# A two-layer gated feed-forward network in float32 on one core: its small inputs packed into two arrays, and one queue for the first layer's base weights

## The chip, the cores and the metric

The kernel runs on one core of a Trainium2 chip. The metric is the device time of one execution in microseconds (us). Before the change, three runs took 442.56, 443.47 and 443.69 us; their median is 443.47 us. One further execution was recorded by the hardware profiler, and every duration below comes from that one.

## What is computed

There are eight sequences (b) of 128 tokens with 512 features. The network has two layers, and each adds its result to x. The part that the change touches is the first layer's condition: a dense product with W, and a low-rank correction by two of eight experts per token. The experts are chosen by logits to which the sequence's language adds 5.

```python
def _L0_cond_ref(x, language_ids, W, Wr, A, B):
    base = jnp.einsum('btd,od->bto', x, W)
    logits = jnp.einsum('btd,ed->bte', x, Wr)
    logits = logits + one_hot(language_ids, E)[:, None, :] * LANG_BIAS
    topw, topi = jax.lax.top_k(logits, TOP_K)
    weights = jax.nn.softmax(topw, axis=-1)
    gates = jnp.sum(jax.nn.one_hot(topi, E) * weights[..., None], axis=-2)
    h = jnp.einsum('btd,erd->bter', x, A)
    lora_out = jnp.einsum('bter,bte,eor->bto', h, gates, B)
    return base + SCALING * lora_out
...
x = x + _L0_ffn_ref(_L0_cond_ref(x, ...), ...)
x = x + _L1_ffn_ref(_L1_cond_ref(x, L1_cond_weight, itok_B_3_7), ...)
```

After the condition come a gated feed-forward with 4-bit weights (scales and zero points by groups of 128 rows), then a second layer: one 512 x 512 weight per sequence, picked by a second list of eight numbers, a root-mean-square norm with weights ln_w, and a gated feed-forward in float32.

## The kernel before, in words

The 1024 tokens are worked on in two halves of 512 columns (tb 0 and 1), features on the 128 partitions in four chunks (c, or m for outputs). A float32 product is made of three passes over parts of the operands: both operands are split into a high part and a scaled rest (x: `x_high`, `x_low`, `x_scaled`; base weights: `w_high`, `w_low`), and a third pass takes their differences (`x_diff`, `w_diff`). ScalarE (ACT) makes the high parts and the scaled rests, VectorE (DVE) the lows and differences.

**Loads.** `wa` (272 KB) holds the weights of the experts' logits and of their first factor A. `xb` is x, eight loads of 256 KB, one per sequence. `wT` holds the base weights, four loads of 256 KB, one per output chunk m. `bT` is the experts' second factor. SyncE (SP) issues `wa`, xb 1, 3, 5 and 7, the eight language numbers `ids0` between xb 3 and xb 5, then wT 0 and 2, `bT`, `shifts`, two parts of `g_idx`, `ids1`, the first quantised weights `qw`, the zero points `qz`, a second `qw`, the scales `sc` and `scd`, `ln_w`, `qzd`, and the residual `xT`. ACT issues xb 0, 2, 4 and 6 at the start (L220), and wT 1 and 3 (L708, through L226) behind `x_high(0)` in its own instruction stream.

In the built program all loads issued by SP and ACT, counted together, carry eight counters in turn. So each of these loads waits, on the engine that issues it, until the load eight places before it has landed. The order of the places before is: xb0, wa, xb2, xb1, xb4, xb3, xb6, ids0; xb5, xb7, wT0, wT2, bT, shifts, g_idx, g_idx; ids1, qw, qz, wT1, wT3, qw, sc, scd; ln_w, qzd, xT, xT, qwd.

**Order of work.** For TensorE (PE), DVE and ACT the order is written out by hand (L702 to L767). PE: `experts(0)` and `experts(1)` (logits and A products of each half), then 16 matmuls of the first base pass of half 0 (L723, four for each m, each m after its `w_high(m)`), the transposes `turned` of the gated values (L724), the second pass of half 0, two passes of half 1, and the third passes, the low-rank products (L416) and the split of the condition (L675, L676) that the gate and up products of the feed-forward read.

```python
exp0 = experts(0)
x_high(0)
for m in range(1, KC, 2):
    load_wT(m, nc.scalar)
x_low(0)
x_scaled(0)
exp1 = experts(1)
for m in range(2):
    w_high(m)
hg0 = gated(0, rows_of(exp0))
for m in range(2, KC):
    w_high(m)
```

`gated` (L306) is a chain of small DVE operations with one Exp on ACT in its middle (L325). ACT works in program order, so that Exp stands behind `w_high(1)`, and the four of `x_scaled(0)` stand behind ACT's two loads. Behind the Exp, DVE does the rest of `gated(0)`, `w_low`, `x_low(1)`, `x_diff(0)`, `w_diff`, `gated(1)`, `x_diff(1)` and the unpacking of the first quantised weights (L425, L428, L445).

A second version of the network, `in_float32` (L828), is in the program for inputs whose groups or scales are unusual; it does not run here.

Of the kernel before, what the change touches and what calls it, by code (L numbers as in the profile page):

```python
# [13 lines left out]
F32 = mybir.dt.float32  # L14
F32R = mybir.dt.float32r
I32 = mybir.dt.int32
U32 = mybir.dt.uint32
U16 = mybir.dt.uint16
# [4 lines left out]
P = 128  # L23
B, T, D = 8, 128, 512
# [40 lines left out]

LINE = 16
GU_PLACE, FLAG_PLACE, COND_PLACE = 64, 24, 48

AFTER = 0.3
FETCHED = [EngineType.PE, EngineType.DVE, EngineType.Activation]  # L70
# [21 lines left out]
def network_in(ctx, tc, a, out, by_groups, flag, again):  # L92
# [116 lines left out]
    wT3 = [cp.tile([P, KC, D], F32R, name=f"wT{i}") for i in range(3)]  # L209
    xd = [cp.tile([P, KC, TB], F32R, name=f"xd{tb}") for tb in range(NTB)]  # L210
    bT = cp.tile([P, D], F32, name="bT")
    wa = cp.tile([P, KC * (E + E * R) + COND_PLACE], F32, name="wa")
    wa = wa[:, : KC * (E + E * R)].rearrange("p (c n) -> p c n", c=KC)
    g_idx = const.tile([P, KC + NJ0], I32, name="g_idx")
    ids = const.tile([P, 2, B], I32, name="ids")
    shifts = const.tile([P, 2], U16, name="shifts")

    nc.sync.dma_start(out=wa, in_=a["WA"])
    for b in range(B):
        (nc.scalar, nc.sync)[b % 2].dma_start(  # L220
            out=xb[:, b].rearrange("p c t -> p (c t)"), in_=a["xb"][b]
        )
        if b == 3:
            nc.sync.dma_start(out=ids[:, 0, :], in_=a["ids0"].partition_broadcast(P))
    def load_wT(m, eng):
        eng.dma_start(out=wT[:, m, :], in_=a["WT"][:, m, :])  # L226

    for m in range(0, KC, 2):
        load_wT(m, nc.sync)
    nc.sync.dma_start(out=bT, in_=a["BT"])  # L230
    nc.sync.dma_start(out=shifts, in_=a["shifts"])
    nc.sync.dma_start(out=g_idx[:, :KC], in_=a["g_idx_gu"])
    nc.sync.dma_start(out=g_idx[:, KC:], in_=a["g_idx_d"])
    nc.sync.dma_start(out=ids[:, 1, :], in_=a["ids1"].partition_broadcast(P))

    def load_residual():
        for c in range(0, KC, 2):
# [15 lines left out]
    make_identity(nc, ident)  # L253
    eps = const.tile([P, 1], F32, name="eps")
    nc.gpsimd.memset(eps, RMS_EPS)
    ln_w = const.tile([P, KC], F32, name="ln_w")

    def in_range(dst, src, n, name):
        wrap = const.tile(list(src.shape), F32, name=f"wrap_{name}")
# [7 lines left out]
    def indices():  # L267
        in_range(idx[:, :KC], g_idx[:, :KC], NG_GU, "gu")
        in_range(idx[:, KC:], g_idx[:, KC:], NG_D, "d")
        lora = const.tile([P, B], F32, name="lora")  # L270
        in_range(lora, ids[:, 1, :], E, "l1")
        nc.vector.scalar_tensor_tensor(
            row1, lora, float(P), iota_p.to_broadcast([P, B]), ALU.mult, ALU.add
        )
# [31 lines left out]
    def gated(tb, banks):  # L306

        nb = TB // T
        ct = lambda shape, name, dt=F32: cp.tile(shape, dt, tag=name, bufs=2, name=name)
        logits = ct([P, nb, E], "logits")  # L310
        tok = ids[:, 0, tb * nb : (tb + 1) * nb, None]
        nc.vector.tensor_tensor(logits, tok.to_broadcast([P, nb, E]), ebc, ALU.is_equal)
        for i, ps in enumerate(banks):
            some = logits[:, 2 * i : 2 * i + 2, :]
            nc.vector.scalar_tensor_tensor(some, some, LANG_BIAS, ps[:, :, :E], ALU.mult, ALU.add)
        top = ct([P, nb, 8], "top")
        topi = ct([P, nb, 8], "topi", U32)
        for b in range(nb):
            nc.vector.max(top[:, b, :], logits[:, b, :])
            nc.vector.max_index(topi[:, b, :], top[:, b, :], logits[:, b, :])  # L320
        w = ct([P, 2, nb, 1], "w")
        dif = ct([P, nb, 1], "dif")
        ex = ct([P, nb, 1], "ex")
        nc.vector.tensor_tensor(dif, top[:, :, 1:2], top[:, :, 0:1], ALU.subtract)
        nc.scalar.activation(ex, dif, AF.Exp)  # L325
        nc.vector.tensor_scalar(dif, ex, 1.0, None, ALU.add)
        nc.vector.reciprocal(dif, dif)
        nc.vector.tensor_scalar(w[:, 0], dif, SCALING, None, ALU.mult)
        nc.vector.tensor_tensor(w[:, 1], w[:, 0], ex, ALU.mult)
        gates = ct([P, nb, E], "gates")  # L330
        second = ct([P, nb, E], "second")
        for n, g in enumerate((gates, second)):
            nc.vector.tensor_tensor(g, topi[:, :, n : n + 1].to_broadcast([P, nb, E]), ebc, ALU.is_equal)
            nc.vector.tensor_tensor(g, g, w[:, n].to_broadcast([P, nb, E]), ALU.mult)
        nc.vector.tensor_tensor(gates, gates, second, ALU.add)
        hg = ct([P, nb, E * R], "hg")
        for i, ps in enumerate(banks):
            some = slice(2 * i, 2 * i + 2)
            nc.vector.tensor_tensor(
                hg[:, some, :].rearrange("p b (e r) -> p b e r", e=E),  # L340
                ps[:, :, E:].rearrange("p b (e r) -> p b e r", e=E),
                gates[:, some, :, None].to_broadcast([P, 2, E, R]),
                ALU.mult,
            )
        return hg
# [107 lines left out]
    def by_groups_of_scales():  # L453
        gu_stack = ExitStack()
        gup = gu_stack.enter_context(tc.tile_pool(name="gup", bufs=1, side="left"))
        sc = const.tile([P, 2 * NJ0, NG_GU], F32, name="sc")
        scd = const.tile([P, KC, NG_D], F32, name="scd")
        qz = gup.tile([P, 2 * 2 * KC * NW + GU_PLACE], U16, name="qz")
        qz = qz[:, GU_PLACE:].rearrange("p (h a w) -> p h a w", h=2, a=2 * KC)
        qws, qwds, wqs, dqs, zqs, wds, h2 = {}, {}, {}, {}, {}, {}, {}  # L460
# [10 lines left out]
            out=qz.rearrange("p h a w -> p (h a w)"), in_=a["qzb_gu"].partition_broadcast(P)  # L471
        )
        load_qw(*PAIRS0[1])
        nc.sync.dma_start(out=sc, in_=a["sc_gu_T"])
        nc.sync.dma_start(out=scd, in_=a["sc_d_T"])
        nc.sync.dma_start(out=ln_w, in_=a["ln_w"])
        qzd = gup.tile([P, NJ0, P], U16, name="qzd")
        nc.sync.dma_start(
            out=qzd.rearrange("p k n -> p (k n)"), in_=a["qzb_d"].partition_broadcast(P)
# [222 lines left out]
        with tc.manual_schedule(engines={EngineType.PE, EngineType.DVE, EngineType.Activation}):  # L702
# [1 line left out]
            nc.scalar.activation(root, eps, AF.Exp)  # L704
            exp0 = experts(0)
            x_high(0)
            for m in range(1, KC, 2):
                load_wT(m, nc.scalar)  # L708
            x_low(0)
            x_scaled(0)  # L710
            exp1 = experts(1)
# [116 lines left out]
    def in_float32():  # L828
        gp_stack = ExitStack()
        ax = gp_stack.enter_context(tc.tile_pool(name="gx", bufs=1, side="left")).tile([P, KC, NT], F32, name="ax")  # L830
        load_residual()
        for m in range(1, KC, 2):
            load_wT(m, nc.scalar)
        scale_bT()
        for m in range(KC):
            for part in (w_high, w_low, w_diff):
# [86 lines left out]
                        )  # L923
                    nc.vector.tensor_tensor(xT[:, m, cols], xT[:, m, cols], ps, ALU.add)
        h_stack.close()
        nc.sync.dma_start(out=ln_w, in_=a["ln_w"])
        pools["w1"] = w1_stack.enter_context(tc.tile_pool(name="w1", bufs=1, side="right"))
        first_w1()
        open_l1()
# [312 lines left out]
def hidden_order(w, axis):  # L1242

    return by_nibbles(w, axis, [16] * KC)
# [64 lines left out]
def chunks(w):  # L1309

    return w.reshape(-1, P, w.shape[1]).transpose(1, 0, 2)
# [4 lines left out]
    return w.reshape(P, KC, KC, P).swapaxes(1, 2).reshape(P, KC, D)  # L1316


def laid_out(i):
    sc = gate_up_order(i["L0_ffn_scales_gu"])  # L1320
    sc_halves = [inner_order(h, 1) for h in (i["L0_ffn_scales_gu"][:, :INTER0], i["L0_ffn_scales_gu"][:, INTER0:])]
    sc_d = x_order(i["L0_ffn_scales_down"], 1)
    qz = pairs(i["L0_ffn_qzeros_gu"])
    qz_d = np.ascontiguousarray(pairs(i["L0_ffn_qzeros_down"])).reshape(NG_D, P)
    g_d = np.pad(inner_order(i["L0_ffn_g_idx_down"], 0), (0, P - CH0[10]), mode="edge")
    gate, up = (i[k].reshape(NJ1, P, KC, P).transpose(0, 3, 2, 1) for k in ("L1_ffn_gate_w", "L1_ffn_up_w"))
    p = np.arange(P)
    d = {
        "xT": x_order(i["x"].reshape(NT, D), 1).T,
        "xb": x_order(i["x"].reshape(NT, D), 1).T.reshape(KC, P, B, T).transpose(2, 1, 0, 3).reshape(B, P, D),  # L1330
        "ids0": i["itok_B_0_7"],
        "ids1": i["itok_B_3_7"],
        "WT": by_chunk(chunks(x_order(hidden_order(i["L0_cond_W"], 0), 1).T)),
        "WA": chunks(
            x_order(np.concatenate([i["L0_cond_Wr"], i["L0_cond_A"].reshape(E * R, D)]), 1).T
        ),
        "BT": hidden_order(i["L0_cond_B"], 1).transpose(0, 2, 1).reshape(E * R, D),
        "shifts": np.stack([4 * (p // 16 % 4), 4 * (p // 12 % 4)], axis=1).astype(np.uint16),
        "qw_gu": by_partition(gate_up_order(i["L0_ffn_qweight_gu"]), [16] * KC),
        "qz_gu0": qz[:, 0],  # L1340
        "qz_gu1": qz[:, 1],
        "qzb_gu": qz.transpose(1, 0, 2).reshape(-1),
        "sc_gu": sc,
        "sc_gu_T": np.stack([by_output(h) for h in sc_halves], axis=2).reshape(P, 2 * NJ0, NG_GU),
        "g_idx_gu": hidden_order(i["L0_ffn_g_idx_gu"], 0).reshape(KC, P).T,
        "qw_d": by_partition(x_order(i["L0_ffn_qweight_down"], 1), [n // 8 for n in CH0]),
        "qz_d": qz_d,
        "qzb_d": np.concatenate([qz_d, qz_d[-1:]]).reshape(-1),
        "sc_d": sc_d,
        "sc_d_T": by_output(sc_d),  # L1350
        "g_idx_d": g_d.reshape(NJ0, P).T,
        "w1": x_order(i["L1_cond_weight"], 2).transpose(0, 2, 1).reshape(E, KC, P, D).transpose(0, 2, 1, 3).reshape(E * P, KC * D),
        "ln_w": i["L1_ffn_ln_w"].reshape(KC, P).T,
        "wgu1": np.stack([gate, up], axis=3).reshape(NJ1, P, KC, 2 * P),
        "wd1": chunks(x_order(i["L1_ffn_down_w"], 0).T),
    }
    return {k: np.ascontiguousarray(v) for k, v in d.items()}
# [17 lines left out]
```

## Time and profile before

| | us |
|---|---|
| median of three runs | 443.47 |
| the profiled execution, its time | 444.12 |
| its span, first to last instruction | 442.3 |
| PE busy in the span | 427.3 (97%) |
| DVE busy | 302.3 (68%) |
| ACT busy | 232.0 (52%) |
| from the start to the first gate product of layer 0 | 50.6 |

The span is counted from the first instruction. Most of it is PE at work; the first 25 us are the stretch in which PE has idle time of microseconds and in which the granted clock falls to half. The DMA queues move 9.68 of the 33.07 MB in the first 60 us. A chain of waits is followed back from the last instruction; a row "DMA wT<-in_WT" in it is the time from a load's issue until it had landed, and "SPq" or "ACTq" is the issuing of a load by that engine.

### The profile page before, as it was taken

The page shows a single profiled execution, that of the slowest core. Times are in us where ns is not written, and L with a number is a line of the kernel's source. Part 1 is how long each engine was busy: PE and PEld are TensorE (multiplying, and loading weights), DVE is VectorE, ACT ScalarE, POOL GpSimd, SP SyncE. Part 2 cuts the span into 40 slices and gives each one's busy share as a digit, 9 for nine tenths or more (in the row PEclk, how much of TensorE's full clock was granted, in tenths as well). Part 3 has the DMA queues.
Part 4 walks back from the last instruction along what each step waited for, and adds up shares of the span by engine and source line. Part 5 has one row for each costly group of instructions (what it writes and reads, how often), then busy time and mean ns, then how long its engine had stood idle before and what let it go on. Part 6 is the DMA issues. An engine that isn't in the chain of part 4 may idle for free.

```text
span 442.3 us, 4852 instructions
## 1 busy us (share of the span) xinstructions
PE 427.3 (97%) x1855; PEld 335.8 (76%) x1855; DVE 302.3 (68%) x432; ACT 232.0 (52%) x269; POOL 9.0 (2%) x20
## 2 busy tenths in 40 slices
PE   8599999999999999999999999999999999999993
PEld 8486678888888866446888888888888888888882
DVE  4298979997999678867449926379626477634652
ACT  3553588867896766346487323475132471325321
POOL 0000000000000200210000000000000000000000
PEclk9799999999999999999999999999999999999997
DMA  7950130101000602870403301112001110000004
GB/s 273 282 217 0 49 96 0 49 19 37 0 0 1 272 13 97 298 270 4 142 1 104 133 1 37 47 50 94 36 0 47 49 48 24 1 0 1 1 31 163
DMA packets 13103, 33.07 MB, mean 75 GB/s; under 512 B 2705, under 2 KB 5265, under 8 KB 12049
## 3 DMA queue, kind: packets, MB, share of 16 engines
q1 hardware_dynamic: 10480, 21.68, 14.7%
q0 software_dynamic: 1152, 8.39, 5.1%
q10 hardware_dynamic: 1440, 2.62, 1.8%
q8 instruction: 16, 0.26, 0.2%
q14 instruction: 15, 0.11, 0.1%
HBM read 30.59 MB, written 2.10 MB: 74 GB/s over the span
## 4 chain that ended last, share of the span: by engine, by line
PE 82%; issue 8%; DMA 7%; ACT 1%; POOL 0%; DVE 0%; ACTq 0%; SPq 0%; POOLq 0%; DVEq 0%
PE gate L1066 17%; PE up L1066 17%; PE down L1131 17%; PE gate L544 7%; PE up L544 7%; PE down L592 7%; PE base L390 5%; DMA w<-in_w,row 3%; DMA wT<-in_WT 3%; PE adapt L1009 2%; PE base L416 2%; DMA xb<-in_xb 1%; POOL w L277 0%; DVE xT L1148 0%; PE nxT L1029 0%
## 5 line engine op out<-in xcount | busy, mean ns | idle before, releaser
L1066 PE MATMUL gate<-a,w 128*128 128x512 f32 x336 | 81.7, 390 | 0.0
L1066 PE MATMUL up<-a,w 128*128 128x512 f32 x336 | 81.4, 389 | 0.0
L1131 PE MATMUL down<-h,d 128*128 128x512 f32 x336 | 76.8, 389 | 0.0
L1066 PEld LDWEIGHTS up<-a,w 128*128 128x128 f32 x336 | 63.1, 188 | 13.1
L1131 PEld LDWEIGHTS down<-h,d 128*128 128x128 f32 x336 | 63.1, 188 | 13.1
L1066 PEld LDWEIGHTS gate<-a,w 128*128 128x128 f32 x336 | 62.7, 188 | 13.5 <-ACT gate L175 0.6
L1083 DVE SCALAR_TENSOR_TENSOR h<-up,sl 128x1024 f32<-128x1024 f32 (+1 forms) x16 | 17.5, 1091 | 50.9 <-PE up L1066 44.5
L544 PE MATMUL gate<-a,dq 128*128 128x512 f32 (+1 forms) x176 | 47.7, 393 | 0.1
L544 PE MATMUL up<-a,dq 128*128 128x512 f32 (+1 forms) x176 | 47.4, 391 | 0.0
L592 PE MATMUL down<-h,wd 128*128 128x512 f32 (+1 forms) x176 | 42.3, 394 | 0.6 <-DVE h L189 0.4
L592 PEld LDWEIGHTS down<-h,wd 128*128 128x128 f32 (+1 forms) x176 | 32.5, 188 | 9.5 <-DVE h L189 0.9
L544 PEld LDWEIGHTS gate<-a,dq 128*128 128x128 f32 (+1 forms) x176 | 32.5, 185 | 8.4 <-ACT sl L560 0.6
L544 PEld LDWEIGHTS up<-a,dq 128*128 128x128 f32 (+1 forms) x176 | 32.4, 185 | 8.0 <-DVE a L676 0.3
L199 ACT ACTIVATE h<-h 128x1024 fp32r<-128x1024 f32 (+1 forms) x25 | 26.4, 1055 | 15.9 <-DVE h L1083 15.5
L1080 ACT ACTIVATE sl<-gate 128x1024 f32<-128x1024 f32 (+1 forms) x16 | 14.7, 918 | 36.0 <-PE gate L1066 36.0
L189 DVE TENSOR_TENSOR h<-h,h 128x1024 fp32r<-128x1024 f32 (+1 forms) x25 | 30.4, 1216 | 3.4 <-ACT h L199 3.4
L175 ACT ACTIVATE gate<-gate,ratio 128x1024 f32<-128x1024 f32 (+1 forms) x24 | 26.1, 1086 | 10.6 <-PE gate L544 10.6
L175 ACT ACTIVATE gate<-gate 128x1024 f32<-128x1024 f32 (+1 forms) x15 | 13.8, 923 | 30.5 <-PE gate L1066 30.5
L1009 PE MATMUL adapt<-w,xT 128*128 128x512 f32 x64 | 28.9, 597 | 0.4 <-DMA w<-in_w,row 0.4
L175 ACT ACTIVATE down<-down 128x1024 f32<-128x1024 f32 (+1 forms) x10 | 9.2, 923 | 35.8 <-PE down L1131 35.8
L175 ACT ACTIVATE up<-up,ratio 128x1024 f32<-128x1024 f32 (+1 forms) x23 | 25.0, 1085 | 5.1 <-PE up L544 5.1
L1148 DVE SCALAR_TENSOR_TENSOR xT<-down,xT 128x1024 f32<-128x1024 f32 (+1 forms) x17 | 19.6, 1160 | 9.3 <-PE down L1131 9.1
(139 smaller groups left out, 485.9 us busy)
## 6 DMA issues: line engine op xcount, KB each, us to landing
wgu<-in_wgu SPq DMA_DIRECT2D x14, 512.0 KB, 3.3
wd<-in_wd SPq DMA_DIRECT2D x6, 512.0 KB, 3.6
qw<-in_qw_gu SPq DMA_DIRECT2D x5, 512.0 KB, 4.1
xT<-in_xT SPq DMA_DIRECT2D x2, 1024.0 KB, 6.4
xb<-in_xb ACTq DMA_DIRECT2D x4, 256.0 KB, 5.4
xb<-in_xb SPq DMA_DIRECT2D x4, 256.0 KB, 5.5
qwd<-in_qw_d SPq DMA_DIRECT2D x2, 512.0 KB, 6.0
out<-xT SPq DMA_DIRECT2D x4, 256.0 KB, 3.0
```

The source lines that it names most:

```text
L175: nc.scalar.activation(ps, ps, AF.Copy, scale=by)
L189: nc.vector.tensor_tensor(lo, x, hi.bitcast(F32), ALU.subtract)
L199: nc.scalar.activation(hi, x, AF.Copy, scale=HSCALE)
L390: nc.tensor.matmul(base[m], lhsT=wT3[i][:, m, c * P : (c + 1) * P], rhs=x_parts(tb)[i][:, c, :], start=(i == 0 and c == 0), stop=(i == 1 a ...
L544: nc.tensor.matmul(ps, lhsT=dqs[j][:, c, half, :], rhs=a3[i][:, c, tb * TB : (tb + 1) * TB], start=(c == 0 and i == 0), stop=(i == 1), ski ...
L592: nc.tensor.matmul(ps[:, tb], lhsT=wds[k][:n, m * P : (m + 1) * P], rhs=h2[k][i][:, tb], start=(first and i == 0), stop=(i == 1), skip_gro ...
L1009: nc.tensor.matmul(ps, lhsT=xT[:, c, b * T : (b + 1) * T], rhs=wt[:, c * D : (c + 1) * D], start=(c == 0), stop=(c == KC - 1),)
L1066: nc.tensor.matmul(ps, lhsT=w3[j][i][:, c, half * P : (half + 1) * P], rhs=a3[i][:, c, tb * TB : (tb + 1) * TB], start=(i == 2 and c == 0) ...
L1080: nc.scalar.activation(sl, ps, AF.Silu, scale=1.0 + EPS)
L1083: nc.vector.scalar_tensor_tensor(h, ps, 1.0 + EPS, sl, ALU.mult, ALU.mult)
L1131: nc.tensor.matmul(banks[m, tb], lhsT=d3[j][i][:, m * P : (m + 1) * P], rhs=h3[j][i][:, tb], start=(i == 0 and j == j0), stop=(j == j1 - 1 ...
L1148: nc.vector.scalar_tensor_tensor(x, ps, -EPS, x, ALU.mult, ALU.add)
```

## The change

The language numbers `ids0` are repeated on every partition and appended to `wa`'s rows, 8 words behind 544, so they come in `wa`'s load. `sc`, `scd`, `ln_w`, both parts of `g_idx`, `ids1` and `shifts` become slices of one tile `small` with one load of 156 words per partition (78 KB). The tile is 176 words wide, 704 bytes; the tiles that it replaces took 64 + 64 + 32 + 32 + 352 + 160 = 704 bytes, so the tiles above it in the pool lie where they lay. All four wT loads are issued by SP directly behind xb 7, and then `bT` and `small`; ACT issues only xb 0, 2, 4 and 6. The order on PE, DVE and ACT is otherwise the same. Packing is done in the layout of the inputs, ahead of the launch.

```diff
+SMALLS = (2 * NJ0 * NG_GU, KC * NG_D, KC, KC + NJ0, B, 1)
+SMALL = 176
...
-    wa = cp.tile([P, KC * (E + E * R) + COND_PLACE], F32, name="wa")
-    wa = wa[:, : KC * (E + E * R)].rearrange("p (c n) -> p c n", c=KC)
-    g_idx = const.tile([P, KC + NJ0], I32, name="g_idx")
-    ids = const.tile([P, 2, B], I32, name="ids")
-    shifts = const.tile([P, 2], U16, name="shifts")
-
-    nc.sync.dma_start(out=wa, in_=a["WA"])
+    wa_ids = cp.tile([P, KC * (E + E * R) + COND_PLACE], I32, name="wa")[:, : KC * (E + E * R) + B]
+    wa = wa_ids[:, : KC * (E + E * R)].bitcast(F32).rearrange("p (c n) -> p c n", c=KC)
+    ids0 = wa_ids[:, KC * (E + E * R) :]
+
+    nc.sync.dma_start(out=wa_ids, in_=a["WA"])
     for b in range(B):
         (nc.scalar, nc.sync)[b % 2].dma_start(
             out=xb[:, b].rearrange("p c t -> p (c t)"), in_=a["xb"][b]
         )
-        if b == 3:
-            nc.sync.dma_start(out=ids[:, 0, :], in_=a["ids0"].partition_broadcast(P))
-    def load_wT(m, eng):
-        eng.dma_start(out=wT[:, m, :], in_=a["WT"][:, m, :])
-
-    for m in range(0, KC, 2):
-        load_wT(m, nc.sync)
+    for m in range(KC):
+        nc.sync.dma_start(out=wT[:, m, :], in_=a["WT"][:, m, :])
     nc.sync.dma_start(out=bT, in_=a["BT"])
-    nc.sync.dma_start(out=shifts, in_=a["shifts"])
-    nc.sync.dma_start(out=g_idx[:, :KC], in_=a["g_idx_gu"])
-    nc.sync.dma_start(out=g_idx[:, KC:], in_=a["g_idx_d"])
-    nc.sync.dma_start(out=ids[:, 1, :], in_=a["ids1"].partition_broadcast(P))
+
+    small = const.tile([P, SMALL], I32, name="small")
+    nc.sync.dma_start(out=small[:, : sum(SMALLS)], in_=a["small"])
+    at = np.cumsum((0,) + SMALLS)
+    sc, scd, ln_w, g_idx, ids1, shifts = (small[:, at[i] : at[i + 1]] for i in range(len(SMALLS)))
...
-        tok = ids[:, 0, tb * nb : (tb + 1) * nb, None]
+        tok = ids0[:, tb * nb : (tb + 1) * nb, None]
...
-        nc.sync.dma_start(out=sc, in_=a["sc_gu_T"])
-        nc.sync.dma_start(out=scd, in_=a["sc_d_T"])
-        nc.sync.dma_start(out=ln_w, in_=a["ln_w"])
...
             x_high(0)
-            for m in range(1, KC, 2):
-                load_wT(m, nc.scalar)
             x_low(0)
```

More of the change, by code (lines that the diff above doesn't have):

```diff
@@ L222, in network_in @@
         )
-        if b == 3:
-            nc.sync.dma_start(out=ids[:, 0, :], in_=a["ids0"].partition_broadcast(P))
-    def load_wT(m, eng):
-        eng.dma_start(out=wT[:, m, :], in_=a["WT"][:, m, :])
-    for m in range(0, KC, 2):
-        load_wT(m, nc.sync)
-    nc.sync.dma_start(out=bT, in_=a["BT"])
-    nc.sync.dma_start(out=shifts, in_=a["shifts"])
-    nc.sync.dma_start(out=g_idx[:, :KC], in_=a["g_idx_gu"])
-    nc.sync.dma_start(out=g_idx[:, KC:], in_=a["g_idx_d"])
-    nc.sync.dma_start(out=ids[:, 1, :], in_=a["ids1"].partition_broadcast(P))
+    for m in range(KC):
+        nc.sync.dma_start(out=wT[:, m, :], in_=a["WT"][:, m, :])
+    nc.sync.dma_start(out=bT, in_=a["BT"])
+    small = const.tile([P, SMALL], I32, name="small")
+    nc.sync.dma_start(out=small[:, : sum(SMALLS)], in_=a["small"])
+    at = np.cumsum((0,) + SMALLS)
+    sc, scd, ln_w, g_idx, ids1, shifts = (small[:, at[i] : at[i + 1]] for i in range(len(SMALLS)))
+    sc = sc.bitcast(F32).rearrange("p (j g) -> p j g", j=2 * NJ0)
+    scd = scd.bitcast(F32).rearrange("p (m g) -> p m g", m=KC)
+    ln_w, shifts = ln_w.bitcast(F32), shifts.bitcast(U16)
     def load_residual():
@@ L255, in network_in @@
     nc.gpsimd.memset(eps, RMS_EPS)
-    ln_w = const.tile([P, KC], F32, name="ln_w")
     def in_range(dst, src, n, name):
@@ L270, in indices @@
         lora = const.tile([P, B], F32, name="lora")
-        in_range(lora, ids[:, 1, :], E, "l1")
+        in_range(lora, ids1, E, "l1")
         nc.vector.scalar_tensor_tensor(
@@ L455, in by_groups_of_scales @@
         gup = gu_stack.enter_context(tc.tile_pool(name="gup", bufs=1, side="left"))
-        sc = const.tile([P, 2 * NJ0, NG_GU], F32, name="sc")
-        scd = const.tile([P, KC, NG_D], F32, name="scd")
         qz = gup.tile([P, 2 * 2 * KC * NW + GU_PLACE], U16, name="qz")
@@ L831, in in_float32 @@
         load_residual()
-        for m in range(1, KC, 2):
-            load_wT(m, nc.scalar)
         scale_bT()
@@ L925, in in_float32 @@
         h_stack.close()
-        nc.sync.dma_start(out=ln_w, in_=a["ln_w"])
         pools["w1"] = w1_stack.enter_context(tc.tile_pool(name="w1", bufs=1, side="right"))
@@ L1316, in by_chunk, with each, words @@
     return w.reshape(P, KC, KC, P).swapaxes(1, 2).reshape(P, KC, D)
+def each(v):
+    return np.broadcast_to(v, (P, len(v)))
+def words(*parts):
+    return np.concatenate([np.ascontiguousarray(x).view("<i4") for x in parts], axis=1)
 def laid_out(i):
@@ L1326, in laid_out @@
     gate, up = (i[k].reshape(NJ1, P, KC, P).transpose(0, 3, 2, 1) for k in ("L1_ffn_gate_w", "L1_ffn_up_w"))
+    wa = chunks(x_order(np.concatenate([i["L0_cond_Wr"], i["L0_cond_A"].reshape(E * R, D)]), 1).T)
     p = np.arange(P)
@@ L1330, in laid_out @@
         "xb": x_order(i["x"].reshape(NT, D), 1).T.reshape(KC, P, B, T).transpose(2, 1, 0, 3).reshape(B, P, D),
-        "ids0": i["itok_B_0_7"],
-        "ids1": i["itok_B_3_7"],
         "WT": by_chunk(chunks(x_order(hidden_order(i["L0_cond_W"], 0), 1).T)),
-        "WA": chunks(
-            x_order(np.concatenate([i["L0_cond_Wr"], i["L0_cond_A"].reshape(E * R, D)]), 1).T
-        ),
-        "BT": hidden_order(i["L0_cond_B"], 1).transpose(0, 2, 1).reshape(E * R, D),
-        "shifts": np.stack([4 * (p // 16 % 4), 4 * (p // 12 % 4)], axis=1).astype(np.uint16),
+        "WA": words(wa.reshape(P, -1), each(i["itok_B_0_7"])),
+        "BT": hidden_order(i["L0_cond_B"], 1).transpose(0, 2, 1).reshape(E * R, D),
+        "small": words(
+            np.stack([by_output(h) for h in sc_halves], axis=2).reshape(P, -1),
+            by_output(sc_d).reshape(P, -1),
+            i["L1_ffn_ln_w"].reshape(KC, P).T,
+            hidden_order(i["L0_ffn_g_idx_gu"], 0).reshape(KC, P).T,
+            g_d.reshape(NJ0, P).T,
+            each(i["itok_B_3_7"]),
+            np.stack([4 * (p // 16 % 4), 4 * (p // 12 % 4)], axis=1).astype("<u2"),
+        ),
         "qw_gu": by_partition(gate_up_order(i["L0_ffn_qweight_gu"]), [16] * KC),
@@ L1343, in laid_out @@
         "sc_gu": sc,
-        "sc_gu_T": np.stack([by_output(h) for h in sc_halves], axis=2).reshape(P, 2 * NJ0, NG_GU),
-        "g_idx_gu": hidden_order(i["L0_ffn_g_idx_gu"], 0).reshape(KC, P).T,
         "qw_d": by_partition(x_order(i["L0_ffn_qweight_down"], 1), [n // 8 for n in CH0]),
@@ L1349, in laid_out @@
         "sc_d": sc_d,
-        "sc_d_T": by_output(sc_d),
-        "g_idx_d": g_d.reshape(NJ0, P).T,
         "w1": x_order(i["L1_cond_weight"], 2).transpose(0, 2, 1).reshape(E, KC, P, D).transpose(0, 2, 1, 3).reshape(E * P, KC * D),
-        "ln_w": i["L1_ffn_ln_w"].reshape(KC, P).T,
         "wgu1": np.stack([gate, up], axis=3).reshape(NJ1, P, KC, 2 * P),
```

## The prediction, made before the changed kernel was run

> **What bounds the kernel now.** I read the page first: PE is busy for 427.3 of 442.3 us, so a change of loads can only win where PE stands still or runs slowly. Then the stretches, cut where PE's work changes. Columns behind the stretch: its length, the busy time of PE, PE's weight loads, DVE, ACT, POOL, then PE's granted clock, DMA share, GB/s.
>
> ```profile
> 4.00:12.83 8.83, 8.41 (x75) 7.98 (x72) 4.37 (x20) 2.54 (x5) 0.00 (x0) 1.00 0.90 291
> 12.83:16.30 3.47, 0.00 (x0) 0.00 (x0) 0.00 (x0) 2.71 (x5) 0.00 (x0) 1.00 1.02 345
> 16.30:18.84 2.54, 1.20 (x5) 0.68 (x5) 0.00 (x0) 0.68 (x3) 0.00 (x0) 0.72 1.01 321
> 18.84:24.33 5.49, 5.49 (x14) 4.22 (x15) 5.18 (x17) 4.30 (x9) 0.00 (x0) 0.51 0.98 320
> 24.33:50.60 26.27, 26.27 (x105) 18.82 (x104) 23.60 (x70) 10.48 (x14) 0.00 (x0) 1.00 0.21 75
> ```
>
> The experts' products end at 12.83. PE then does nothing for 3.47 us, four base products and another gap, and twelve more at half clock. From 24.33 it never stops. The chain that ended last, in order of time (start, length, what), says why:
>
> ```profile
> 6.12 5.56 DMA wT<-in_WT
> 11.67 0.02 issue
> 11.69 6.44 DMA wT<-in_WT
> 18.13 0.02 issue
> 18.16 0.64 ACT wT L377
> 18.80 0.04 issue
> 18.84 5.49 PE base L390 x12
> 24.33 0.46 PE experts L410 x4
> 24.79 14.84 PE base L390 x64
> ```
>
> It runs through two base weight loads, one issued only when the other had landed. ACT's timeline shows where (start, length; in brackets the idle time before and its end):
>
> ```profile
> 7.87 0.63 ACT L359 ACTIVATE a<-xb 128x512 fp32r<-128x512 f32 x1 [1.40 <-DMA xb<-in_xb]
> 11.69 1.80 ACTq L226 DMA_DIRECT2D wT<-in_WT  x2
> 13.54 2.19 ACT L369 ACTIVATE a<-a 128x512 fp32r<-128x512 f32 x4 [5.05 <-issue]
> 15.64 0.61 ACT L377 ACTIVATE wT<-wT 128x512 fp32r<-128x512 f32 x1
> 18.16 0.63 ACT L377 ACTIVATE wT<-wT 128x512 fp32r<-128x512 f32 x1 [1.91 <-DMA wT<-in_WT]
> 18.69 0.19 ACT L325 ACTIVATE ex<-dif 128x4 f32<-128x4 f32 x1
> 20.20 0.63 ACT L377 ACTIVATE wT<-wT 128x512 fp32r<-128x512 f32 x1 [0.80 <-DMA wT<-in_WT]
> ```
>
> ACT is done with x_high(0) at 8.50, then idles 5.05 us in front of its own two loads, which wait for the loads eight places ahead (wT2, landed at 11.67; bT, issued at 8.05, landed 4.3 later at 12.35). All of x_scaled, w_high and the Exp queue behind that. DVE waits 7.7 us for the Exp (waits view).
>
> **Part 1, the base weights on SP: when they land.** In the new order ids0 leaves its place, so xb5 is eighth and goes out in the first burst near 2.1 instead of at 4.40. The rest wait eight places back, on landings worked out from issue plus time to landing: xb7 on xb0 (4.35), wT0 on wa (4.24), wT1 on xb2 (5.7), wT2 on xb1 (5.3, but SP is in order, so about 6.1), wT3 on xb4 (8.05). Before, SP's successive 256 KB loads xb7, wT0, wT2, bT landed at 10.5, 11.06, 11.67, 12.36, a step of 0.55 to 0.7. Now wT0 to wT3 follow xb7 in that row. At the old pace they land at 11.06, 11.67, 12.36, 13.0. Early bound: about 1 us sooner, because the DMA rate sags to some 190 GB/s from 6 to 8 us and xb5 can fill that. Late bound: the time that wT1 and wT3 took beside qw and qz, 6.4 and 7.8 us after issue, that is 12.2 and 15.9. I take the old pace, the nearest row: same sizes, same queue, no quantised weights beside them.
>
> **ACT.** Its two issues (1.80 us) and the wait go. x_scaled(0) follows x_high(0): 8.50 + 2.19 = 10.7 (its last input, x_low, ends at 9.22). w_high(0) 11.06 to 11.7, w_high(1) to 12.3, Exp to 12.5 (its input is ready at 11.17), w_high(2) to 13.1, w_high(3) to 13.8.
>
> **PE.** At full clock a base product takes 14.84 / 64 = 0.232 us, so from 12.83 the four groups want their weights at 12.83, 13.76, 14.69 and 15.61. They are ready at 11.7, 12.3, 13.1, 13.8: at least 1.1 us of slack each. The pass then ends at 12.83 + 16 x 0.232 = 16.54 instead of 24.33: 7.8 us. Of these, 4.8 are the two PE waits for w_high (3.5 and 1.3), and 3.0 are half clock and small gaps. The clock needs its own check. The Trainium skill, "TensorE: Matmul & The Clock Gate", section "What's actually happening", has half rate after an idle window of about 3.4 us and full rate after one busy window of that length. The trace has a gap of 3.47, half rate soon after, and full rate only near 24.2, 5.4 us into unbroken work (18.84). If a gap that size stayed, the page would price the restart at half of 3.4, 1.7 us; the row prices it at 5.49 - 12 x 0.232 = 2.7. With no gap left, I take neither: full clock, as in 4.00:12.83.
>
> **What is late next.** Behind the Exp, DVE works without a pause from 18.88 to 41.34 (22.46 us); it then waits 1.15 for ACT's split of the condition, and 0.50 before the next one at 44.22. With the Exp's end at 12.5 it is done at 35.0. PE, 7.8 earlier, lets ACT split at 33.65, and its first part is out at 34.7. DVE is 0.3 late there, and the 0.50 takes it up; up to an Exp's end of about 12.7 nothing is lost, and beyond it each us of the Exp costs PE one. ACT: the kept copy, x_high(1), scaling of bT and hgT end at about 17.8; PE wants x_high(1) at 20.7 (ready at 16.6) and x_scaled(1) at 24.4 (ready near 20.4). The hg values, 2.5 us behind the Exp, are there at 15.0, wanted at 16.54. I take 0.1 off for all this: 7.7.
>
> **Part 2, the packed inputs.** Eight loads go, one comes: SP's issue rows for the eight add up to 4.0 us (0.33 to 1.07 each), against one of about 0.45, plus 2 x 0.4 for the two wT. The skill, "DMA: Bandwidth & Descriptors", "Rules for kernel authors", calls transfers under 64 KB mostly overhead and asks for one large one; its section on the anatomy of one DMA gives about 2.0 us fixed each. By that rule seven fewer would be 14 us. The trace has 3.6 to 8.1 us from issue to landing for each, but no engine row waits for any of their contents: they overlap, and what they take is places among the eight. So in this sum they are worth nothing by themselves. What hides small: it goes out when xb6 has landed (about 9.2) and lands by 17.3 even at sc's 8.1; its first reader, shifts at 39.55, moves to about 32. Without that cover each us past 32 would cost one. wa's rows grow from 544 to 552 words, 1.5% of 3.5 us: 0.05, inside the 0.1 between wa's landing (4.24) and xb0's (4.35).
>
> **Part 3, what moves behind.** SP's row is now xb7, four wT, bT, small, qw, qz, qw, qzd, xT, qwd. Bytes are nearly the same, in less time. qz and qw took 7.2 to 8.9 us to land; issued near 10.5 to 11.5, they are there by 20, and DVE wants them at about 31.5 and 33. qwd, issued after xT, landed at 29.3 before and is wanted at 50.1. xb5 in the first burst shares engines with xb3 and xb4. xb3 stands ahead of it in SP's row, so I take no change; bounds: 0.4 earlier (PE's wait at 7.89 is 0.42) to 0.6 later (one place in the row), and either moves everything. Behind 50.6, loads wait for buffers that engines release, so they move along; nothing there gives or takes.
>
> **The sum.** Span 442.3 - 7.7 = 434.6; the profiled execution, 444.12 with 1.8 around its span, 436.4. It lay 0.65 above the median, so against the median of 443.47: 435.8.
>
> **The rivals.**
> 1. As summed: 435.8; its own range 435.0 to 436.8. Chance 0.79.
> 2. The weights stay slow, at the late bound: wT3 at 15.9, w_high(3) out at 16.5 instead of by 15.61: 0.9 lost, and 0.6 more if xb3 is late too: 437.3. For it: wT1 and wT3 did take that long. Against: qw and qz were beside them. Chance 0.10.
> 3. DVE becomes the bound. The Exp stands behind w_high(1); if wT1 lands at 13.8, 8.1 us after issue (the slowest small load's time), the Exp ends at 14.6 and 1.9 us are lost: 437.7. Chance 0.06.
> 4. It doesn't do what it says: w_high(0) still comes after 16.2, the gap is over 3.4 us and the clock falls: 443.5. Chance 0.02; wT0 would have to land 5 us later than now.
> 5. Slower: the quantised inputs starve. qz is now behind all base weights in one in-order queue, and DVE's unpacking stops until it lands. Each us after 31.5 is a us of PE's; it decides from 31.5 + 7.7 = 39.2. At 41 the time is 445.3. Against it: about 4.4 MB through qz at the 380 GB/s of busy slices are 12 us. Chance 0.03.
>
> Range: 434.6 to 437.8; it takes in cases 1 to 3. A measurement here can tell about 0.3% (1.3 us) from no change. Cases 1 to 3 are faster by more; with a little on each side, faster 0.95, same 0.02, slower 0.03.
>
> **What would show it.** Right: no wT load on ACT's queue and no idle time before L369; wT3 landed by about 13; base products unbroken from 12.83 to 16.5 at clock 1.00; first gate product near 42.8; no new PE wait for DVE before that. Wrong: a PE wait for w_high in the first pass; Exp ending after 12.7 with PE waiting for L676; xb3 landing well off 7.85; DVE waiting for qz or qw.

## The result, and the profile after

Six executions of each kernel: 443.49 us before (median, 442.56 to 444.84), 436.89 us after (436.04 to 437.84). The ratio is 0.985, 95% interval 0.9829 to 0.9871, 6.6 us less. The profiled execution after took 436.83 us, with a span of 434.9. Among the executions below, one of before (875.84 us), one of e1 (723.06) and one of e4 (1314.49) were slow; the ratios leave them out, and without them the medians of e1 and e4 are 441.71 and 442.08.

The stretches after, cut at the same times as before (columns as there: length, busy PE, PE's weight loads, DVE, ACT, POOL, granted clock, DMA share, GB/s):

```profile
4.00:12.83 8.83, 8.54 (x75) 8.34 (x73) 4.82 (x23) 6.44 (x14) 0.00 (x0) 1.00 1.01 354
12.83:16.30 3.47, 3.47 (x18) 2.83 (x18) 3.30 (x12) 3.47 (x7) 0.00 (x0) 1.00 1.02 332
16.30:18.84 2.54, 2.54 (x15) 2.08 (x14) 2.54 (x5) 1.73 (x4) 0.00 (x0) 1.00 0.92 320
18.84:24.33 5.49, 5.49 (x25) 4.44 (x24) 5.49 (x11) 3.25 (x5) 0.00 (x0) 1.00 0.99 400
24.33:50.60 26.27, 26.27 (x103) 18.51 (x103) 24.42 (x69) 11.73 (x13) 0.00 (x0) 1.00 0.19 62
```

PE is busy in every part from 12.83 on, and the clock is full. The chain that ended last (start, length, what) no longer passes a base weight:

```profile
1.65 6.56 DMA xb<-in_xb
8.21 0.04 issue
8.25 4.90 PE experts L293 x40
13.15 3.73 PE base L390 x16
16.89 0.44 PE experts L410 x4
17.33 14.83 PE base L390 x64
```

Its only load is xb3, landed at 8.21. The first base pass ends at 16.89 instead of 24.33, 7.44 us sooner, and the span is 7.4 shorter. ACT's timeline after:

```profile
8.23 0.63 ACT L359 ACTIVATE a<-xb 128x512 fp32r<-128x512 f32 x1 [1.56 <-DMA xb<-in_xb]
8.77 2.17 ACT L369 ACTIVATE a<-a 128x512 fp32r<-128x512 f32 x4
10.87 1.32 ACT L377 ACTIVATE wT<-wT 128x512 fp32r<-128x512 f32 x2
12.10 0.19 ACT L325 ACTIVATE ex<-dif 128x4 f32<-128x4 f32 x1
12.19 1.24 ACT L377 ACTIVATE wT<-wT 128x512 fp32r<-128x512 f32 x2
```

There is no load issue in it and no idle time behind 8.23. All four splits are out by 13.43, while PE wants the last at about 15.9.

### The profile page after: what moved, and what is told of

Same layout as the page of the kernel before. It is cut to its first block, busy times and chain, and to the rows that moved or that the text cites. A ratio compares the mean times of both kernels' runs of the same rounds, so it can differ in the third digit from the quotient of the medians.

```text
span 434.9 us, 4847 instructions
## 1 busy us (share of the span) xinstructions
PE 424.8 (98%) x1855; PEld 334.5 (77%) x1855; DVE 302.4 (70%) x432; ACT 232.0 (53%) x269; POOL 9.0 (2%) x20
## 4 chain that ended last, share of the span: by engine, by line
PE 91%; DVE 4%; DMA 2%; ACT 1%; issue 0%; SPq 0%; ACTq 0%; DVEq 0%
PE gate L1056 18%; PE up L1056 18%; PE down L1121 17%; PE gate L539 9%; PE down L587 8%; PE up L539 8%; PE base L390 5%; PE adapt L999 5%; PE base L416 2%; DMA xb<-in_xb 2%; PE experts L293 1%; DVE xT L599 1%; PE nxT L1019 1%; ACT sl L555 1%; DVE h L558 1%; DVE w L952 1%
## 5 line engine op out<-in xcount | busy, mean ns | idle before, releaser
L203 ACT ACTIVATE h<-h 128x1024 fp32r<-128x1024 f32 (+1 forms) x25 | 26.4, 1054 | 15.9 <-DVE h L1073 15.5
```

The costliest lines, as they stand in the source:

```text
L203: nc.scalar.activation(hi, x, AF.Copy, scale=HSCALE)
```

## The experiments

My theory after the result: the gain is all in the moment at which base weights 1 and 3 are issued and so landed, and the packing brings nothing of it. Rivals: the packing counts through the places among the eight; ACT's idle time is the cost; SP's single queue is what helps; the half clock has another cause. A question beside them was why the medians differ by 6.6 us and the two profiles by 7.3.

**e1, the packing alone.** ACT keeps its two loads.

```diff
-    for m in range(KC):
+    for m in range(0, KC, 2):
         nc.sync.dma_start(out=wT[:, m, :], in_=a["WT"][:, m, :])
...
             x_high(0)
+            for m in range(1, KC, 2):
+                nc.scalar.dma_start(out=wT[:, m, :], in_=a["WT"][:, m, :])
```

> The packed inputs of the change, but base weights 1 and 3 stay with ACT, behind x_high(0). The prediction priced the packing at nothing by itself: then the time is that of before, 443.5 us, with ACT idle about 5 us in front of its loads. The rival: the small loads took places among the eight, and with them gone ACT's two loads wait for xb7 and wT0 (landed near 10.2 and 10.9) instead of wT2 and bT (11.7 and 12.4). Then ACT is held only until about 11.7, the second weight lands near 16.5 and the first base pass ends near 19.8 instead of 24.3: about 4.5 us of the 7.4, 439 us, clock probably full because PE's first gap is under 2 us.

Measured: 441.87 us, ratio 0.996 (0.9945 to 0.9974); span 439.5. From the chain of waits of e1:

```profile
9.11 6.91 DMA wT<-in_WT
16.05 0.64 ACT wT L377
16.73 4.42 PE base L390 x12
21.15 0.44 PE experts L410 x4
```

Both sides missed. The packing is not worth nothing when it stands alone: with the small loads out of the places ahead, wT1 is issued at 9.11 instead of 11.69 and lands at 16.02 instead of 18.13. But the pass ends at 21.15, not at 19.8, because the clock fell after all (half rate from 16.33 to 19.74).

**e2, the four weights on SP alone**, behind xb7, with the small inputs in their eight loads.

```diff
-    for m in range(0, KC, 2):
+    for m in range(KC):
         load_wT(m, nc.sync)
...
-            for m in range(1, KC, 2):
-                load_wT(m, nc.scalar)
```

> The kernel of before with all four base weights issued by SP behind xb7, the small inputs in their eight loads as before. My theory: this alone brings the whole gain, because what cost the time was ACT's stream standing before its own two loads; xb5 stays in the ninth place, so xb3 lands at 7.9 as before: first base pass unbroken from 12.8 to 16.5, span 434.5, median 436.2 to 436.8, not slower than the changed kernel. The rival, that the small loads' places and SP's issue time also count: qw, qz and the scales come later and 1 to 3 us of the gain are missing (437.5 to 440).

Measured: 436.69 us, ratio 0.9845 (0.9822 to 0.9869); span 433.9. The first pass is unbroken from 12.69 to 16.42:

```profile
12.69 3.73 PE base L390 x16
```

This is the changed kernel's time, within intervals that are about 1 us wide on either side. So the move of the two loads brings the gain, and the packing adds nothing to it that can be measured.

**e3, small in the eighth place.**

```diff
         )
+        if b == 3:
+            nc.sync.dma_start(out=small[:, : sum(SMALLS)], in_=a["small"])
...
-    nc.sync.dma_start(out=small[:, : sum(SMALLS)], in_=a["small"])
```

> The changed kernel with the load of small in the eighth place, between xb3 and xb5, so that xb5 waits for xb0's landing again. Theory: xb5 in the first burst shares the engines with xb3 and made it land 0.36 us later (8.21 for 7.86), which moved everything; here xb3 is back near 7.9 and the span is 0.3 to 0.4 shorter than the changed kernel's 434.9, a difference too small for the medians. Rival: the 0.36 is chance from one execution to the next, or small's own 78 KB delay xb3 as much; then xb3 stays at 8.2.

Measured: 436.14 us, ratio 0.9831 (0.9811 to 0.9851); span 434.4. xb3 was there by 7.20. That looks like the theory, but in e1, where xb5 is in the first burst as in the change, xb3 was there by 7.10. The theory that xb5 delays xb3 is not borne out; e7 says the same.

**e4, the gap filled.** The kernel of before, with idle products in the gap.

```diff
             pairs0, base0 = base_sums()
+            for _ in range(56):
+                nc.tensor.matmul(base0[3][:, :P], lhsT=ones, rhs=ones, start=True, stop=True)
```

> The kernel of before with its loads, and 56 idle 128x128 products in the gap between the experts' products and the first base product, written to a bank that the base products then clear. It changes nothing but PE's activity. Theory: the half clock is the gap's doing, so the clock stays at 1.00 and the three groups behind the second weight take 0.93 each instead of 1.7, bounded by w_high(3) at 20.8: the pass ends near 21.8 instead of 24.3, about 2.5 us less, 441.0 us. Rival: the low clock has another cause (the weights' arrival pattern or the second gap), then it stays and so does the time, 443.5.

Measured: 442.13 us, ratio 0.9969 (0.9955 to 0.9984), 1.4 us less; span 439.7. Its stretches:

```profile
12.83:16.30 3.47, 3.47 (x61) 3.45 (x60) 0.00 (x0) 2.71 (x5) 0.00 (x0) 1.00 0.95 331
16.30:18.84 2.54, 1.30 (x6) 0.77 (x5) 0.19 (x2) 0.98 (x3) 0.00 (x0) 1.00 1.03 357
18.84:21.90 3.06, 3.06 (x17) 2.49 (x16) 2.85 (x12) 3.06 (x7) 0.00 (x0) 1.00 1.05 381
```

PE still waits for the second weight (1.30 busy of 2.54), but the clock stays at 1.00, and the twelve products behind it take 3.05 us (18.54 to 21.59) instead of 5.49. So the half clock is the gap's doing. Against the first profile of before that is 2.6 us of span, as expected; in the medians it is 1.4. The medians are the better price: a second trace of the kernel of before (e8) ends its pass at 21.77 without any filling, almost as early as this one.

**e5, ACT issues early.** The changed kernel, with weights 1 and 3 on ACT behind xb6.

```diff
     for m in range(KC):
-        nc.sync.dma_start(out=wT[:, m, :], in_=a["WT"][:, m, :])
+        (nc.sync, nc.scalar)[m % 2].dma_start(out=wT[:, m, :], in_=a["WT"][:, m, :])
```

> The changed kernel, but ACT issues base weights 1 and 3, behind xb6 and ahead of all its arithmetic. Theory: what the change wins is the place of the two issues in ACT's stream, not the queue; ACT stands before its loads only until xb0 and xb2 have landed (about 4.5 and 5.7), while it would wait for x anyway, so the first base pass is again unbroken behind the experts' products: span 434 to 435.5, median within 0.3% of the changed kernel. Rival, SP's single queue is needed: ACT's first splits come 1 us later, the weights share the engines with xb5 and xb7 and make the second half's x late; then PE gets gaps of 1 us or more and the time is 438 or above.

Measured: 436.17 us, ratio 0.9838 (0.9812 to 0.9864); span 434.4, the pass unbroken from 13.22 to 16.95. ACT's first arithmetic on x started at 7.52, 3.1 us later than before, and the experts' products took 8.03 us (7.50 in e2), but the median shows no loss. Which queue issues the loads makes no difference that can be measured; the moment of issue does.

**e6, fewer idle products**, on top of e3.

```diff
-NWARM = 37
+NWARM = 30
```

> The kernel with small in the eighth place, and 30 idle products in place of 37 at the start. In four of the six traces so far the idle products end near 5.2, 0.4 to 0.6 after the first x and wa landed, so the experts' products start late. Theory: they start near 4.6 to 4.8, and as PE is unbroken behind, the span falls by 0.3 to 0.5 to about 434.0, unless x3 then holds PE (it landed between 6.9 and 8.2 so far), in which case nothing is won. Rival: with fewer idle products the clock is still low when the experts' products start and the span grows by up to 1 us.

Measured: 436.79 us, ratio 0.9853 (0.9828 to 0.9877); span 434.1. The experts' products start at 4.48 at full clock, and then PE waits 0.2 us for xb3 (7.75). Nothing is won that can be measured.

**e7 and e8, the two kernels once more**, without an edit.

> The changed kernel once more. It shows how much one execution differs from the next: whether xb3's landing (8.21 before, 7.1 in the other runs) and the end of the idle products (5.1) repeat. Theory, these are chance: xb3 near 7.1 to 7.9 and a span of 434 to 435; rival, the change delays xb3: it is at 8.0 or later again. Median 436 to 437 either way.

> The kernel of before once more. Its first profile lay 0.6 us above the median. Theory: the length of the stall (first base pass ended at 24.3) differs between executions with the landing of the two weights that ACT issues, and a typical execution ends it 0.5 to 1 us sooner; then the gain of the change in a typical execution is 6.6, as the medians say, and not the 7.4 of the two profiles. Rival: the pass ends at 24.3 again, and the 0.8 us lie elsewhere in the span.

Measured: e7 436.11 us, ratio 0.9839 (0.9813 to 0.9864), 7.3 us less this time; span 435.1. xb3 was there by 7.60, so the change does not fix it at 8.21. The pass ended at 16.31, 0.58 sooner than in the first profile, yet the span is 0.2 longer; of the 0.8 us lost behind the pass, 0.4 is a PE wait for a gathered weight of the second layer, which the first profile of before has too, and the rest is not explained. e8 442.68 us, ratio 0.999 (0.9974 to 1.0006); its span is 439.6, 2.7 us less than the first profile of the same kernel. This trace is of a short execution (441.40, below the median of 442.68), while the first lay above its median. Its chain:

```profile
12.21 7.49 DMA wT<-in_WT
19.71 0.64 ACT wT L377
20.40 1.37 PE base L390 x4
21.77 0.44 PE experts L410 x4
```

The pass ended at 21.77 there and at 24.33 in the first profile. wT1 was split at 16.21 instead of 18.16, and the clock was low for half the time (the stretch on either side of its return; e8 first, then the first profile of before):

```profile
17.30:20.70 3.40, 3.28 (x9) 2.07 (x8) 3.19 (x13) 1.14 (x3) 0.00 (x0) 0.51 0.97 331
20.70:22.00 1.30, 1.30 (x9) 1.08 (x8) 1.30 (x3) 1.30 (x4) 0.00 (x0) 0.96 0.87 195
```

```profile
17.40:24.20 6.80, 5.46 (x14) 4.09 (x14) 5.05 (x16) 4.98 (x10) 0.00 (x0) 0.50 0.99 329
24.20:25.00 0.80, 0.80 (x7) 0.75 (x6) 0.80 (x3) 0.18 (x1) 0.00 (x0) 0.97 1.03 425
```

So the stall that the change removes has no fixed length: single executions of before spread from 440.31 to 445.19 us, those of the changed kernel from 435.95 to 437.84. The mean granted clock over the whole execution, recorded for 113 executions of before, goes with the time: the 16 at 0.992 or more took 441.4 us on average, the 11 at 0.984 or less 444.5.

**e9, ACT's loads behind x_scaled(0)**, in the kernel of before.

```diff
             x_high(0)
-            for m in range(1, KC, 2):
-                load_wT(m, nc.scalar)
             x_low(0)
             x_scaled(0)
+            for m in range(1, KC, 2):
+                load_wT(m, nc.scalar)
```

> The kernel of before, with ACT's two weight loads moved behind x_scaled(0), so that ACT no longer stands idle for 4 to 5 us in front of its arithmetic. The loads themselves are issued no earlier: they wait for bT and shifts (landed near 12.4). Theory: the landing of the two weights sets the end of the first base pass, not ACT's idle time. Then w_high(0) is ready near 13.9 instead of 16.2, but wT1 lands near 18.5 and wT3 near 20, PE stands idle between them, the clock falls all the same, and the pass ends between 22 and 24.5: no gain of the size of the change, 442 to 444.5 us. Rival: ACT's idle time is what cost, then 3 to 5 us go, 438.5 to 440.5.

Measured: 444.07 us, ratio 1.0018 (1.0005 to 1.003); span 444.2. ACT's timeline:

```profile
8.86 2.17 ACT L369 ACTIVATE a<-a 128x512 fp32r<-128x512 f32 x4
12.41 0.84 ACTq L226 DMA_DIRECT2D wT<-in_WT  x2
13.30 0.63 ACT L377 ACTIVATE wT<-wT 128x512 fp32r<-128x512 f32 x1 [2.26 <-DMA shifts<-in_shifts]
20.05 0.63 ACT L377 ACTIVATE wT<-wT 128x512 fp32r<-128x512 f32 x1 [6.12 <-DMA wT<-in_WT]
```

x_scaled(0) no longer waits behind the loads and the first weight is split 2.3 us sooner than before, yet the second waits until 20.05 and the pass ends at 26.22. So taking away ACT's 5.05 us of idle time, the largest figure in the ACT rows shown of before, wins nothing as long as the loads come no earlier: the landing of wT1 sets the end. The test is not a clean one. In this trace wT1 was issued 0.7 us later than in the first profile of before (12.41) and landed 1.9 later, and the traced execution (446.10) is the second longest of its 22; the median, 0.6 us above that of before, is what bears the conclusion.

## Why the prediction held, and where it was off

- **The forecast was 435.8, the measured time 436.9, inside the range; forecast gain 7.7, measured 6.6.** The step that was off is the last one of the sum, "It lay 0.65 above the median, so against the median of 443.47: 435.8". The profiled execution of before was above the median and its stall was a long one (in e8 the pass ends 2.6 us sooner, and behind the pass the two traces take 417.97 and 417.83 us). The change removes the stall, so what is left does not inherit its length. The sum in the profiled execution's own terms, 436.4, was already the time after, and it is half a microsecond from the 436.83 and 436.92 of the two profiled executions. By taking the 7.7 off the median I subtracted 0.65 us twice. In the first profile 0.36 of the remaining 0.43 is xb3's later landing. The repeat of the changed kernel (e7) came to 436.11, so medians of five or six executions settle such remainders only to some tenths.
- **xb3 "no change".** It landed at 8.21 instead of 7.86, inside the bounds I gave (0.4 earlier, 0.6 later). In the runs it was there between 6.97 and 8.33, and both kinds of run, with and without xb5 in the first burst, are spread over most of that: chance, as far as these single traces show, not the change.
- **The landings.** wT0 to wT3 were said to be there at 11.06, 11.67, 12.36 and 13.0. In the profile after, the first was issued at 4.87 and took 6.0; the last landed 4.4 after an issue at 8.4, at 12.8. The old pace was the right row. The late bound (rival 2), taken from loads with quantised weights beside them, did not come about, nor did rival 3: the Exp ended at 12.29 (12.5 forecast), and PE waited for DVE no more than before.
- **The clock.** That full clock would hold with no gap left was right. The price of the half clock, 2.7 us, is that of one long execution: half rate lasted 6.83 us there, 3.41 in e8. Filling the gap (e4) was worth 1.4 us in the medians.
- **"In this sum they are worth nothing by themselves"** (the packed inputs). For this change it held: e2 has the gain without them. Taken alone the sentence was wrong: e1 gains 1.8 us by the places that the eight small loads leave. The two parts attack the same wait, and whichever comes first takes it. The page's count for the fixed cost of seven loads, 14 us, showed nowhere; its section gives the 2.0 us for loads that GpSimd issues, and these are issued by SP.
- **What moves behind.** Nothing gave the gain back: from the end of the first pass to the end of the span it is 417.97 us before and 418.0 after (418.8 in e7). Part 3 held, and so did rival 5's low chance: qz was issued at 10.7, landed in 6.8, and DVE began on it at 31.3.

## What to carry to other kernels

Where loads share a few counters in turn, a load's place in the issue order sets when it can start; ask of every late load which earlier landing its issue waits for, before its size or its queue. An idle engine in front of such a load is not yet a cost: move the wait (e9), and see whether the landing behind it sets the end anyway. When a change removes a stall that differs from one execution to the next, forecast the time after from the profiled execution itself, and do not carry the difference over to a median.

## What the runs showed of the hardware

- **PE's clock changed on a grid of 3.41 us.** Half rate in the first part of the execution lasted 3.41 us in e8 and e1, 6.83 in the first profile of before (17.41 to 24.24) and 10.24 in e9 (16.13 to 26.37): one, one, two and three times 3.41. From its return the clock stayed full until PE's last work was done; it then fell at 437.23, 436.17, 437.25 and 439.38, which is 122.0, 122.0, 121.0 and 121.0 times 3.413 us after the return. This agrees with the free-running window of 3.4 us of the Trainium skill ("TensorE: Matmul & The Clock Gate", "What's actually happening").
- **It fell with no gap of 3.4 us**: in e8 after gaps of 2.79 us (12.69 to 15.48) and 0.21, in e1 after gaps of 1.38 and 0.99 us with 1.20 us of work between them. In the window of the grid that ended with the fall, PE was busy for 33% (before), 42% (e1), 50% (e8) and 51% (e9) of the time; after windows of 62% (e8) and 66% (before) the clock stayed. The page has half rate after an idle window; none of these four was idle. The busy share alone is not the rule either, since near the end of e8 and e2 windows of 43% and 45% left the clock full. What the limit is stays open.
- **At half rate**, windows in which PE was busy for 0%, 61% and 65% did not bring full clock back; windows of 88%, 96% and 100% did. So a wait that ends late in a window can cost a whole window more; that this tells the four lengths apart fits these traces and was not tested by itself. The window before the fall in e1, the one that lifted the clock again, and one in e9 that did not:

```profile
12.92:16.33 3.41, 1.44 (x7) 0.72 (x5) 0.00 (x0) 1.85 (x5) 0.00 (x0) 1.00 1.03 398
16.33:19.74 3.41, 3.01 (x7) 2.43 (x8) 2.70 (x12) 2.49 (x6) 0.00 (x0) 0.50 1.07 405
19.54:22.95 3.41, 2.22 (x5) 1.82 (x6) 1.90 (x11) 2.90 (x7) 0.00 (x0) 0.50 0.97 324
```

- Loads of 256 KB took from 3.6 to 8.1 us to land, and the same load (xb3) differed by 1.4 us from one trace to another.
